# Self attention on one Trainium2 core: a table of orders, one for each batch, block and position

## The chip, the cores and the metric

The kernel runs on one core of one Trainium2 chip. The metric is the device time of one execution in microseconds. All data are 32-bit floats.

## The reference

A decoder block reads `x` (2 x 2048 x 512) and a short encoded context (2 x 77 x 512). Cut to what matters here:

```python
sb = _rel_bias(dec_rel_self, Tt, Tt) + causal        # bias by distance, and the causal mask
y = tgt
yn = _ln(y, dec_n1_s, dec_n1_b)
y = y + _mha(yn, yn, dec_sa_in_w, dec_sa_in_b, dec_sa_out_w, dec_sa_out_b, sb)   # self attention
y = y + _mha(_ln(y, dec_n2_s, dec_n2_b), memory, ...)                            # cross attention
h = _ln(y, dec_n3_s, dec_n3_b)
y = y + (relu(h @ dec_ff1_w.T + dec_ff1_b) @ dec_ff2_w.T + dec_ff2_b)

# in _mha, 16 heads of 32:
scores = einsum('bhqd,bhkd->bhqk', q, k) / sqrt(hd) + bias
attn = softmax(scores, axis=-1)
out = einsum('bhqk,bhkd->bhqd', attn, v)
```

The change touches the self attention alone: causal, two batches, 2048 positions, 16 heads.

## The kernel before

**Units.** The self attention is cut into 128 *units* `(b, m, g, t)`: batch `b`, block `m` of 512 queries, group `g` of four heads, and position `t`, one of four tiles of 128 queries in the block. A unit's queries see `m * 4 + t + 1` tiles of 128 keys, so the blocks grow: a unit of `m = 0` has 1 to 4 key tiles, one of `m = 3` has 13 to 16. Units run in order, `t` fastest, `b` slowest.

**What a unit does.** (1) *Scores* (`scores`, L375): in *pieces* of up to four key tiles, TensorE multiplies queries and keys. The four heads of the group use 32 rows of the array each, side by side, and each head has a PSUM bank of its own, so a piece takes four banks. VectorE moves each bank to SBUF and takes the row maximum on the way (L384, and L391 for the last two key tiles, which get the bias). (2) *Exponentials* (L406): one ScalarE instruction for each head, when the whole row is there. (3) *Transposes* (`turn`, L427): for each key tile TensorE transposes the four heads' probabilities into one bank, and ScalarE (L434) or VectorE (L432) copies the bank to `pts`, a ring of eight tiles. (4) *Values* (`values`, L456): TensorE multiplies the transposed probabilities and the values, each head in 32 columns of the array, into a bank that is taken out of the ring for as long as the sum is open. L469 (ScalarE) copies the sum to `oT`, or L471 (VectorE) adds it there, if the unit's key tiles come in more than one half.

**Banks.** PSUM's eight banks are one ring (`bank()`): whoever needs a bank gets the one used longest ago, and waits until that one has been emptied.

**Slots.** Between the units stands other work in *slots*: `slot(n)` runs the functions in `light[n]` (loads, normalizations, reciprocals of sums, transposes of the input at L305 with ScalarE's copies at L310), then the products in `jobs[n]` (queries, keys, values and the output's projection: L215, L226, L239, and in pieces L1049, L1134, with VectorE's sums at L1056 to L1065, L1150, L1164), then `late[n]`. Each job first asks for the next weights, three to four jobs ahead. In batch 1, blocks 0 and 1, the slots also hold the first piece of the cross attention (L811 to L883).

**What sets the order.** The scheduler is off (`tc.manual_schedule()`): each engine executes in the order in which the program's text issues. A main loop goes through the stream of score pieces. In each turn it takes a unit's next one or two pieces and issues: their transposes; a fixed number of exponentials of the next unit, by block; with the unit's last pieces, the slot of the next unit; one or two score pieces of the unit after the next, if `may_score()` says that their place in SBUF is free (two units share the buffer `pp`, one growing from each end); the values. The rules are the same for both batches, and for all positions but for some counts:

```python
            third = units[n][1] == 2
            if third and ends:
                exps(2)
            if ends and n + 1 < end:
                slot(n + 1)
            if not third:
                exps((0, 2, 1, 1)[units[n][1]])
            if may_score():
                if units[n][1] and (len(pair) > 1 or third):
                    score_two()
                else:
                    score_next()
```

After the units come the rest of the cross attention and the feed-forward part, whose lines (L1638, L1667, L1758, L1801) the change does not touch.

## Time and profile before

| | |
|---|---|
| time, median of 3 runs | 2726.79 us (2725.84 to 2729.86) |
| profiled execution: span | 2726.8 us; the page gives no time outside the span |
| busy: TensorE, its weight loads | 2708.1 us (99%), 2217.9 us (81%) |
| busy: VectorE, ScalarE, GpSimd | 1839.9 (67%), 1537.0 (56%), 1002.4 us (37%) |
| self attention (all units) | 0 to about 1640 us of the span |
| granted TensorE clock, mean | 0.997 |
| DMA | 385.10 MB, mean 141 GB/s |

A matmul counts as busy from its start to the modelled end of its result, so matmuls that follow each other overlap, and a busy TensorE is not one that works at its peak. On TensorE's rows of 32-bit matmuls each instruction but a transpose leaves two records. The blocks of the self attention begin at 0 (b = 0, m = 0), 161.6, 369.6, 589.5 (m = 1, 2, 3), 853.5 (b = 1, m = 0), 989.7, 1184.2 and 1404.3 us (m = 1, 2, 3), counted by the first transpose of a block.

### The profile page before, as it was taken

The numbers are of one execution on the slowest core, as the hardware profiler recorded it, in microseconds if no ns is written. First come the engines' busy times: TensorE is split into PE (matmuls) and PEld (weight loads), VectorE is DVE, ScalarE is ACT, GpSimd is POOL, SyncE is SP. The second block draws the span as 40 slices with busy tenths as digits, with TensorE's granted clock in tenths as the row PEclk, the third lists the DMA queues.
The fourth block names the chain that finished last, engine by engine and source line by source line (L and its number), as shares of the span: only waits on it lengthen the run. The fifth ranks groups of instructions, "written<-read, shape, count | busy, mean of one in ns | idle before, by whom it ended". The sixth has DMA issues, their size and how long they took to land.

```text
span 2726.8 us, 68267 instructions
## 1 busy us (share of the span) xinstructions
PE 2708.1 (99%) x26606; PEld 2217.9 (81%) x26606; DVE 1839.9 (67%) x5445; ACT 1537.0 (56%) x2978; POOL 1002.4 (37%) x844
## 2 busy tenths in 40 slices
PE   9999999999999999999999999999999999999998
PEld 6678877777876677777777777898989898989898
DVE  4776688888885677788888783646464746464645
ACT  3554567777786547667777784444444444444431
POOL 2612235500300513322300203455556565656456
PEclk9999999999999999999999999999999999999999
DMA  8724355511213522343311206565657565656465
GB/s 242 213 92 135 126 155 164 168 50 43 67 45 89 143 76 72 111 133 98 126 50 35 79 19 220 171 214 173 213 171 239 168 216 170 218 166 219 151 224 185
DMA packets 296277, 385.10 MB, mean 141 GB/s; under 512 B 41184, under 2 KB 165648, under 8 KB 295826
## 3 DMA queue, kind: packets, MB, share of 16 engines
q1 hardware_dynamic: 295954, 380.73, 44.1%
q8 instruction: 211, 3.46, 0.5%
q14 instruction: 112, 0.92, 0.1%
HBM read 334.15 MB, written 46.47 MB: 140 GB/s over the span
## 4 chain that ended last, share of the span: by engine, by line
PE 95%; DVE 1%; ACT 1%; DMA 1%; POOL 1%; issue 1%; SPq 0%; DVEq 0%; POOLq 0%; ACTq 0%
PE psum L427 18%; PE psum L1638 14%; PE psum L1667 13%; PE psum L375 11%; PE psum L456 9%; PE psum L1134 8%; PE psum L1801 3%; PE psum L1758 3%; PE psum L1049 3%; PE psum L866 2%; PE psum L836 1%; PE psum L874 1%; PE psum L590 1%; PE psum L811 1%; PE psum L239 1%; PE psum L215 1%
## 5 line engine op out<-in xcount | busy, mean ns | idle before, releaser
L406 ACT ACTIVATE pp<-pp,nm 128x128 f32<-128x128 f32 (+15 forms) x512 | 611.8, 1200 | 28.6 <-DVE nm L401 27.8
L384 DVE TENSOR_SCALAR_CACHE_REDUCE pp<-psum 128x512 f32<-128x512 f32 (+3 forms) x1024 | 556.2, 591 | 51.3 <-PE psum L375 49.7
L434 ACT COPY pts<-psum 128x512 f32<-128x512 f32 x714 | 384.1, 594 | 312.6 <-PE psum L427 265.6
L427 PE MATMUL psum<-ident,pp 128*128 128x128 f32 x4352 | 530.4, 277 | 4.7 <-ACT nT L310 4.0
L427 PEld LDWEIGHTS psum<-ident,pp 128*128 128x128 f32 x4352 | 474.0, 141 | 55.7 <-DVE pp L384 21.4
L375 PE MATMUL psum<-kT,q 32*128 32x512 f32 (+3 forms) x2560 | 336.5, 559 | 2.5 <-DVE q L217 1.0
L456 PEld LDWEIGHTS psum<-pts,vv 128*32 128x32 f32 x8704 | 226.4, 110 | 127.4 <-DVE pp L384 55.4
L1667 PE MATMUL psum<-pp 128*128 128x128 f32 x2560 | 304.5, 276 | 1.9 <-POOL pp L962 1.6
L1667 PEld LDWEIGHTS psum<-pp 128*128 128x128 f32 x2560 | 296.3, 192 | 8.6 <-issue 2.8
L432 DVE COPY pts<-psum 128x512 f32<-128x512 f32 x374 | 245.2, 685 | 82.6 <-PE psum L427 80.3
L456 PE MATMUL psum<-pts,vv 128*32 128x128 f32 x8704 | 279.6, 276 | 0.8 <-DVE mx L391 0.3
L962 POOL TENSOR_TENSOR pp<-pp 128x512 f32<-128x512 f32 x159 | 212.8, 1356 | 111.0 <-DMA pp<-in_dec_ff_wT_dram 50.6
L1638 PE MATMUL psum<-vv,pp 128*128 128x256 f32 x1024 | 236.2, 381 | 0.0
L375 PEld LDWEIGHTS psum<-kT,q 32*128 32x128 f32 x2560 | 146.3, 183 | 107.1 <-issue 41.3
L1638 PEld LDWEIGHTS psum<-vv,pp 128*128 128x128 f32 x1024 | 190.3, 190 | 25.8 <-issue 0.5
L391 DVE CUSTOM_DVE_ANT_0 pp<-psum,bias 128x256 f32<-128x256 f32 (+1 forms) x512 | 196.0, 411 | 19.7 <-PE psum L375 19.7
L1651 DVE TENSOR_TENSOR kT<-kT,psum 128x512 f32<-128x512 f32 x96 | 65.8, 686 | 191.6 <-PE psum L1638 191.4
L1654 ACT ACTIVATE kT<-kT,vecs 128x256 f32<-128x256 f32 x192 | 86.9, 501 | 156.6 <-DVE kT L1651 155.9
L1638 PE MATMUL psum<-nT,pp 128*128 128x256 f32 x768 | 174.1, 380 | 0.5 <-DVE oT L471 0.5
L1638 PEld LDWEIGHTS psum<-nT,pp 128*128 128x128 f32 x768 | 144.2, 190 | 20.8 <-issue 1.4
L1675 ACT COPY oT<-psum 128x128 f32<-128x128 f32 x56 | 15.0, 268 | 238.9 <-PE psum L1667 238.9
L494 POOL TENSOR_TENSOR oT<-rirows,oT 128x512 f32<-128x512 f32 x30 | 38.4, 1280 | 293.6 <-DMA rirows<-rec 181.7
(272 smaller groups left out, 4110.6 us busy)
## 6 DMA issues: line engine op xcount, KB each, us to landing
pp<-w_d SPq DMA_DIRECT2D x520, 256.0 KB
pp<-in_dec_ff_wT_dram SPq DMA_DIRECT2D x112, 256.0 KB
bias<-tzg SPq DMA_DIRECT2D x128, 128.0 KB
pp<-wo_d SPq DMA_DIRECT2D x56, 256.0 KB
wqk<-in_dec_sa_in_wT_dram SPq DMA_DIRECT2D x52, 256.0 KB
wqk<-sa_q SPq DMA_DIRECT2D x84, 128.0 KB
vv<-in_enc_ff_wT_dram SPq DMA_DIRECT2D x8, 1024.0 KB
xr<-in_x_dram SPq DMA_DIRECT2D x32, 256.0 KB
```

Of the source, the lines that this page charges most:

```text
L375: nc.tensor.matmul(banks[r][:, : kn * P], q[rows4(r), ts(t, P)], kT[rows4(r), g, k0 * P : (k0 + kn) * P], start=True, stop=True,)
L384: nc.vector.tensor_scalar(p[:, k0 : k0 + far], s[:, :far], 1.0, None, ALU.mult, ALU.max, accum_out=st["mx"][:, r, c : c + 1],)
L391: nc.vector.tensor_tensor_reduce(p[:, k0 + far : i + 1], s[:, far:kn], near[:, 2 - (kn - far) :], 1.0, LOWEST, ALU.add, ALU.max, accum_out ...
L406: nc.scalar.activation(p, p, AF.Exp, bias=nm, accum_out=to)
L427: nc.tensor.transpose(pt[:, ts(x, P)], state[n]["p"][r][:, k], ident)
L432: nc.vector.tensor_copy(pts[:, : len(load), :], pt[:, :w])
L434: nc.scalar.copy(pts[:, : len(load), :], pt[:, :w])
L456: nc.tensor.matmul(ot[rows4(r)], vv[:, k, ts(g * HC + r, HD)], got.pop((n, k, r)), start=k == k0 and (whole or not begun), stop=k == k1 - ...
L962: engine.tensor_tensor(out, a, b, ALU.subtract)
L1134: nc.tensor.matmul(mm[:, ts(f, TOK)], left[:, c, ts(f, P)], right[:, c, :], start=c == 0, stop=c == 1,)
L1638: nc.tensor.matmul(mm[:, ts(f, TOK)], a[:, c, ts(f, P)], b[:, c, :], start=fresh and f == 0 and c == 0, stop=c == 1, skip_group_check=True,)
L1667: nc.tensor.matmul(psum[:, bank_i, ts(col, P)], lhs[:, c, :], w[:, c, :], start=fresh and k in (0, 3) and c == 0, stop=c == 3, skip_group_ ...
```

## The change

The main loop's rules are replaced by a table. For each batch, each block from `m = 1` on and each position `t` a line of letters is the order in which the unit is issued: `a` and `d` transpose the next key tile and copy it on ScalarE or VectorE; `E` issues one exponential of the next unit; `S` one score piece, where its place is free, the second piece of a row first if both are; `V` multiplies what was transposed by the values and closes the sum; `v` does that and leaves the sum open in its bank; `J` issues what is left of the next slot and `j` only its front (`light`). `slot` is split into parts for that. Blocks `m = 0` keep their order, and the last two units have one made by a rule (`script_of`). `turn` takes one tile and the engine that copies it; `values` takes a list of key tiles and whether the sum closes. `may_score` also looks at the places in `pp` that are still held (`held_by`, `leave`). No computation is added or left out but for this: 18 transposed tiles more are copied by VectorE and 18 fewer by ScalarE, and 15 additions of value sums on VectorE (L471) are gone, since batch 0's block 3 keeps its sums open between the halves.

In the new text the transposes are L417, the values L441, the copies L423 (ScalarE), the sums' copy L454, the slots' products L1035 and L1120, and the cross attention's L822, L860, L869.

*Place 1: TensorE in batch 0, block m = 3, heads' group 2, from the slot inside the unit t = 0 to the scores inside t = 1.* Before:

```order
L1134 MATMUL psum<-wqk,oT 128x256 x4
L375 MATMUL psum<-kT,q 128x384 x4
L375 MATMUL psum<-kT,q 128x512 x4
L456 MATMUL psum<-pts,vv 32x128 x20
L427 MATMUL psum<-ident,pp 128x128 x32
L375 MATMUL psum<-kT,q 128x512 x8
L456 MATMUL psum<-pts,vv 32x128 x32
L427 MATMUL psum<-ident,pp 128x128 x24
L305 MATMUL psum<-ident,xt 128x128 x4
L375 MATMUL psum<-kT,q 128x512 x8
L456 MATMUL psum<-pts,vv 32x128 x24
```

and in the changed kernel:

```order
L1120 MATMUL psum<-wqk,oT 128x256 x4
L375 MATMUL psum<-kT,q 128x512 x4
L441 MATMUL psum<-pts,vv 32x128 x20
L375 MATMUL psum<-kT,q 128x384 x4
L417 MATMUL psum<-ident,pp 128x128 x32
L375 MATMUL psum<-kT,q 128x512 x8
L441 MATMUL psum<-pts,vv 32x128 x32
L417 MATMUL psum<-ident,pp 128x128 x24
L375 MATMUL psum<-kT,q 128x512 x4
L305 MATMUL psum<-ident,xt 128x128 x4
L441 MATMUL psum<-pts,vv 32x128 x24
L375 MATMUL psum<-kT,q 128x512 x4
```

The pair of pieces behind the slot's products (L1134, L305) is split: one piece stands ahead of the values, or of the slot, and the other behind the values. The pair behind 32 transposes stays a pair.

*Place 2: ScalarE at the same units (from the exponentials inside t = 1 on).* Before:

```order
L406 ACTIVATE pp,sums<-pp,nm 128x15x128 x2
L469 COPY oT<-psum 128x128
L434 COPY pts<-psum 128x512 x3
L406 ACTIVATE pp,sums<-pp,nm 128x15x128
L310 ACTIVATE nT<-psum,vecs 128x128 x4
L406 ACTIVATE pp,sums<-pp,nm 128x15x128
L434 COPY pts<-psum 128x512 x6
```

and in the changed kernel:

```order
L406 ACTIVATE pp,sums<-pp,nm 128x15x128 x2
L423 COPY pts<-psum 128x512 x3
L406 ACTIVATE pp,sums<-pp,nm 128x15x128 x2
L310 ACTIVATE nT<-psum,vecs 128x128 x4
L454 COPY oT<-psum 128x128
L423 COPY pts<-psum 128x512 x6
```

Both exponentials now stand ahead of the copies of the slot's transposes (L310), and the unit's value sum is copied once, at its end.

*Place 3: TensorE in batch 1, block m = 1, group 0, inside the unit t = 0 and on to the values inside t = 1.* Before:

```order
L375 MATMUL psum<-kT,q 128x384 x4
L375 MATMUL psum<-kT,q 128x512 x4
L456 MATMUL psum<-pts,vv 32x128 x20
L427 MATMUL psum<-ident,pp 128x128 x24
L883 MATMUL psum<-vv,kT 128x512 x4
L836 MATMUL psum<-pp 128x77 x16
L1134 MATMUL psum<-wqk,xt 128x256 x4
L1134 MATMUL psum<-wqk,nT 128x256 x4
L375 MATMUL psum<-kT,q 128x512 x8
L456 MATMUL psum<-pts,vv 32x128 x24
```

and in the changed kernel:

```order
L375 MATMUL psum<-kT,q 128x384 x4
L375 MATMUL psum<-kT,q 128x512 x4
L441 MATMUL psum<-pts,vv 32x128 x20
L869 MATMUL psum<-vv,kT 128x512 x4
L822 MATMUL psum<-pp 128x77 x16
L1120 MATMUL psum<-wqk,xt 128x256 x4
L1120 MATMUL psum<-wqk,nT 128x256 x4
L417 MATMUL psum<-ident,pp 128x128 x24
L375 MATMUL psum<-kT,q 128x512 x4
L441 MATMUL psum<-pts,vv 32x128 x24
L375 MATMUL psum<-kT,q 128x512 x4
```

The slot's four groups of products come ahead of the unit's transposes instead of behind them; the scores no longer stand behind the slot, and their second piece comes behind the values.

Over the whole self attention TensorE's list holds the same instructions. It has 195 runs of score pieces before and 246 after, and 192 runs of values in both; TensorE goes from full-array work (transposes, products) to tiled work (scores, values, the cross attention's heads) 200 times before and 228 times after. In the blocks from `m = 1` on, of 158 runs of scores before, 66 are pairs behind a slot's products, 58 are pairs behind transposes and 34 are single pieces; of 209 after, 5, 68 and 136.

The diff, cut to its core (of the table four lines are shown):

```diff
-        def turn(pieces):
-
-            first = units[pieces[0][0]][1] == 0
...
-                free = pieces[0][0] == len(units) - 2 and (pieces[0][1] or o >= 4)
-                if free or (o % 2 if first else o in (4, 6) if len(loads) == 8 else o >= (len(loads) + 1) // 2):
-                    nc.vector.tensor_copy(pts[:, : len(load), :], pt[:, :w])
-                else:
-                    nc.scalar.copy(pts[:, : len(load), :], pt[:, :w])
-                if not first and o == (7 if len(loads) == 8 else min(3, len(loads) - 1)):
-                    exps(1)
-            exps(HC if first else 0 if units[pieces[0][0]][1] == NMB - 1 else 1)
+        def turn(load, by):
...
+            if by == "d":
+                nc.vector.tensor_copy(pts[:, : len(load), :], pt[:, :w])
+            else:
+                nc.scalar.copy(pts[:, : len(load), :], pt[:, :w])
...
-            keep = t < TB - 1 if whole else (g, t) == (2, 0) and k1 <= i
+            keep = t < TB - 1 if whole else not closes or (g, t) == (2, 0) and not ends
...
+            return [front] + [lambda k=k, run=run: job(k, run) for k, (_, run, _) in enumerate(jobs[n])] + [back]
...
+        SCRIPTS = {
+            (0, 1, 0): 'a a a d E d S E J E E S S V S',
...
+            (0, 3, 1): 'a a a a d a d a E E S S v S a a a d E d d S E J V S',
...
+            (1, 1, 1): 'J a a S a d d E d J E E E S V S S',
...
+            (1, 3, 2): 'j a a a a a d a d E E S S V S a a a a E d d E d J S S V S',
...
+        def may_score(ahead=0):
+
+            if at[0] + ahead >= len(stream):
+                return False
+            n, k0, kn = stream[at[0] + ahead]
+            if any(k in held_by for k in places(n, k0, kn)):
+                return False
...
+            for step in script_of(n):
+                if step in ("a", "d"):
+                    k = to_turn.pop(0)
+                    turn([(n, k, r) for r in range(HC)], step)
+                    turned.append(k)
+                    assert len(turned) <= pts_all.shape[1]
+                    leave(n, k)
+                elif step == "E":
+                    exps(1)
+                elif step == "J":
+                    while parts:
+                        parts.pop(0)()
+                elif step == "j":
+                    parts.pop(0)()
+                elif step == "S" and may_score() and stream[0][0] <= n + 2:
+                    two = stream[0][1] == 0 and may_score(1) and stream[1][0] == stream[0][0]
+                    score_next(1 if two else 0)
+                elif step in ("v", "V"):
+                    values(n, turned, not to_turn, step == "V")
+                    turned = []
```

More of the change, by code (lines that the diff above doesn't have):

```diff
@@ L1891, in tile_encoder_decoder @@
         slot(0)
[L1892 to L1896 removed]
+        for n in range(end):
+            b, m, g, t = units[n]
+            while scored_to[n] != size[n]:
                 score_next()
```

151 lines of the change are left out of this document (69 added, 82 removed), and 20 rows, old and new, of the table SCRIPTS.

## The prediction

> **What bounds the kernel now.** I read the page first, then the windows of the eight blocks, then the score line alone in the same windows, and last TensorE in order of time. The page:
>
> ```profile
> span 2726.8 us, 68267 instructions
> PE 2708.1 (99%) x26606; PEld 2217.9 (81%) x26606; DVE 1839.9 (67%) x5445; ACT 1537.0 (56%) x2978; POOL 1002.4 (37%) x844
> ```
>
> TensorE is the bound, and 99% leaves no idle time to win. But a matmul counts as busy until its result is out, and several overlap, so a wait shorter than that hides inside "busy". The question is how much of the 2708 us is waiting in disguise, in the part that the change reorders. The profiled execution's span is the median of the runs (2726.8 against 2726.79 us), so the sum is made against 2726.8.
>
> Four of the six blocks that are reordered (second column: length; then PE, PEld, DVE, ACT, POOL busy; clock; DMA share; GB/s):
>
> ```profile
> 161.60:369.60 208.00, 207.47 (x2090) 168.88 (x2089) 145.67 (x514) 111.95 (x232) 50.28 (x40) 1.00 0.39 124
> 369.60:589.50 219.90, 219.80 (x2657) 171.37 (x2656) 182.30 (x625) 160.15 (x276) 84.81 (x71) 1.00 0.48 144
> 589.50:853.50 264.00, 263.55 (x3426) 206.83 (x3420) 206.40 (x688) 206.76 (x323) 30.81 (x24) 1.00 0.16 48
> 989.70:1184.20 194.50, 194.43 (x2052) 147.20 (x2048) 145.78 (x499) 128.63 (x267) 55.62 (x47) 0.99 0.29 91
> ```
>
> The clock is full. VectorE, which empties the score banks, is at most 83% busy (182.30 of 219.90), ScalarE 78% (206.76 of 264.00): neither is the bound of a block, so what TensorE waits for there is a matter of order, not of rate. The score line alone in the same windows (all eight blocks; the first and fifth are the blocks m = 0, which keep their order):
>
> ```profile
> 0.00:161.60 161.60, 19.85 (x160) 8.18 (x160) 0.99 0.69 201
> 161.60:369.60 208.00, 34.19 (x273) 15.52 (x272) 1.00 0.39 124
> 369.60:589.50 219.90, 50.47 (x401) 21.53 (x400) 1.00 0.48 144
> 589.50:853.50 264.00, 61.51 (x464) 27.51 (x464) 1.00 0.16 48
> 853.50:989.70 136.20, 17.88 (x144) 7.06 (x144) 0.97 0.47 133
> 989.70:1184.20 194.50, 42.50 (x276) 18.15 (x272) 0.99 0.29 91
> 1184.20:1404.30 220.10, 50.55 (x401) 21.53 (x400) 1.00 0.32 105
> 1404.30:1640.00 235.70, 59.55 (x448) 26.85 (x448) 1.00 0.16 52
> ```
>
> The blocks m = 1 of the two batches do the same scores with the same number of matmuls, yet cost 34.19 and 42.50 us: eight microseconds of waiting in one block, with PE shown 99% busy. TensorE in order of time tells where (start, length, engine, group; a score piece is 8 matmul records, two for each head):
>
> ```profile
> 373.11 1.14 PE L375 MATMUL psum<-kT,q 32*128 32x512 f32 x8
> 374.18 1.74 PE L456 MATMUL psum<-pts,vv 128*32 128x128 f32 x56
> ...
> 741.18 2.77 PE L375 MATMUL psum<-kT,q 32*128 32x384 f32 x16
> 743.88 1.30 PE L456 MATMUL psum<-pts,vv 128*32 128x128 f32 x40
> 745.11 3.71 PE L427 MATMUL psum<-ident,pp 128*128 128x128 f32 x32
> 748.75 2.00 PE L375 MATMUL psum<-kT,q 32*128 32x512 f32 x16
> 750.68 1.96 PE L456 MATMUL psum<-pts,vv 128*32 128x128 f32 x64
> 752.56 2.84 PE L427 MATMUL psum<-ident,pp 128*128 128x128 f32 x24
> 755.24 0.60 PE L305 MATMUL psum<-ident,xt 128*128 128x128 f32 x4
> 755.77 2.09 PE L375 MATMUL psum<-kT,q 32*128 32x512 f32 x14
> 758.19 1.12 PE L375 MATMUL psum<-kT,q 32*128 32x512 f32 x2 [0.34 <-ACT nT L310]
> 759.24 1.52 PE L456 MATMUL psum<-pts,vv 128*32 128x128 f32 x48
> ```
>
> **The price of a run of scores.** From start to the next group's start, two 512-wide pieces in one run take 750.68 - 748.75 = 1.93, one alone 374.18 - 373.11 = 1.07. So a piece costs 0.86 and a run 0.21 more, once, however long it is. In busy time (2.00 and 1.14) the piece is 0.86 too and the run 0.28. Narrower pieces are taken in proportion: 0.645 (384 wide), 0.43, 0.215.
>
> **How much of the score line is waiting.** Its groups by width:
>
> ```profile
> L375 PE MATMUL psum<-kT,q 32*128 32x512 f32 x1600 | 240.1, 616 | 1.6 <-DVE q L217 1.0 <-ACT nT L310 0.3
> L375 PE MATMUL psum<-kT,q 32*128 32x384 f32 x448 | 58.2, 524 | 0.0
> L375 PE MATMUL psum<-kT,q 32*128 32x256 f32 x448 | 44.1, 426 | 0.6 <-DVE kT L1164 0.5
> L375 PE MATMUL psum<-kT,q 32*128 32x512 f32 (+3 forms) x2560 | 336.5, 559 | 2.5 <-DVE q L217 1.0 <-DVE kT L1164 0.5 <-ACT nT L310 0.5
> L427 PE MATMUL psum<-ident,pp 128*128 128x128 f32 x4352 | 530.4, 277 | 4.7 <-ACT nT L310 4.0 <-DVE wbig L1150 0.2
> ```
>
> The last row is the transposes, for later. The first three, divided by 8, are 200 pieces of 512, 56 of 384, 56 of 256, and of the remaining 64 records 8 of 128: 172.0 + 36.1 + 24.1 + 1.7 = 233.9 us. TensorE's order has 195 runs of scores: 195 x 0.28 = 54.6. Undisturbed it would be 288.5; the row has 336.5. So **48 us are waits**. The two windows m = 0 hold 19.85 + 17.88 = 37.7: their 38 pieces (304 records; one of each width in each of eight groups, 17.2, and six of the next blocks, 3.5) and 37 runs (10.4) account for 31.1, so 6.6 us wait there. **41.4 us wait in the six blocks that are reordered.**
>
> They sit in one place. Of the 158 runs of those blocks, 66 are pairs right behind the products of a slot, 58 are pairs behind transposes and 34 are single pieces. The pair at 748.75, behind transposes, waits for nothing. The pair at 741.18 (384 and 512 wide, behind products) takes 2.70 where 0.645 + 0.86 + 0.21 = 1.72 are due: 0.98 of waiting. That at 755.77 takes 3.47 for 1.93. What held it stands on ScalarE:
>
> ```profile
> 754.74 1.92 ACT L406 ACTIVATE pp<-pp,nm 128x1920 f32<-128x1920 f32 x1
> 756.63 1.51 ACT L310 ACTIVATE nT<-psum,vecs 128x128 f32<-128x128 f32 x4
> ```
>
> The eight banks go round in turn. A pair needs all eight, the last being that of the product issued just ahead; here that bank is emptied by L310, queued behind an exponential, until 758.14, and the last score starts at 758.19. I put all 41.4 us on the 66 pairs, 0.63 each.
>
> **The change, part by part.**
>
> *Splitting the pairs (the gain).* In the new order 5 pairs stand behind products, 68 behind transposes, and 136 pieces are alone: ahead of the slot, ahead of the values or behind them. A single piece takes the four oldest banks, and its partner comes after the values or the slot, at least 1.2 us later (the L456 rows). 5 x 0.63 = 3.2 us stay; the 68 pairs wait for nothing. For a single piece the ends are nothing, as at 373.11, and what the row below shows, a piece of 256 behind values:
>
> ```profile
> 1170.88 0.92 PE L375 MATMUL psum<-kT,q 32*128 32x256 f32 x8
> ```
>
> It is busy 0.92 for 0.43 + 0.28 = 0.71: 0.21 of waiting. It comes third behind a pair, when VectorE is four banks further behind than it will be in the new order, so I take the middle, 0.10: 13.6 us for 136 (0 to 28.6). Left are 16.8, and 41.4 - 16.8 = **24.6 us go**.
>
> *More runs (the price).* 209 runs instead of 158: 51 x 0.21 = 10.7. And 28 more times TensorE leaves full-array work for a tiled one: 32 transposes ended by scores take 748.75 - 745.11 = 3.64, 24 ended by other transposes 755.24 - 752.56 = 2.68, which is 3.57 for 32, so 0.07 each time, 2.0 in all. **Price 12.7 us**, certain, because nothing hides work on TensorE itself. The values keep their 192 runs.
>
> *Copies, sums, exponentials.* 18 transposed tiles more are copied by VectorE, and 15 additions of value sums go, because batch 0's last block keeps its sums in a bank across both halves:
>
> ```profile
> L434 ACT COPY pts<-psum 128x512 f32<-128x512 f32 x714 | 384.1, 594 | 312.6 <-PE psum L427 265.6
> L432 DVE COPY pts<-psum 128x512 f32<-128x512 f32 x374 | 245.2, 685 | 82.6 <-PE psum L427 80.3
> L471 DVE TENSOR_TENSOR oT<-psum,oT 128x128 f32<-128x128 f32 x60 | 16.9, 282 | 3.6 <-PE psum L456 2.6 <-ACT pp L406 0.9
> ```
>
> VectorE: 18 x 0.685 - 15 x 0.282 = +8.1 us over six blocks; ScalarE: -18 x 0.594 = -10.7. With a sixth of VectorE idle in its fullest block this costs nothing; without that cover it would be 8.1 us. The held bank leaves seven to the ring between the halves; a single piece and a slot's product still find theirs free.
>
> *Slots moved ahead.* In batch 1, block m = 1, each slot's products, loads and normalizations come before the transposes rather than behind them. The loads keep their place among the jobs, and once started the distance from slot to slot is as before; only the first slot comes sooner, by a run of transposes (2.8 to 3.7 us in the L427 rows). Late weights there would cost at most that, once; I take nothing. What is queued behind: VectorE's sums of the products, which the next transposes need not wait for, since ScalarE copies most of the first ones. This is the block with 8 us more waiting than its twin, and the place of the largest single gain.
>
> **Sum.** -24.6 + 12.7 = -11.9: 2726.8 - 11.9 = **2715 us**. With the single pieces' ends, 0 and 0.21, it is 2701 and 2729.
>
> **The rivals.**
>
> *The singles find every bank free.* The gain is 38.2, net 25.5: **2701**. For it: 373.11, and that a single piece needs only banks that are long done. Against: exponentials of up to 1.9 us now stand closer to a slot's copies on ScalarE in batch 0's last block. 0.17.
>
> *The gain is eaten by its price.* If the lone pieces wait 0.21 as at 1170.88, 31.8 us stay, 9.6 go, and 12.7 are paid: **2729**, no change that shows (a measurement of this kernel cannot tell under 0.2%, 5.5 us, from none). 0.19.
>
> *The waits are a matter of rate, and stay.* VectorE frees a 512-wide bank in 0.61 us while TensorE fills four in 0.86. If the order of the pieces does not matter to that backlog, the 41 us turn up elsewhere, at the transposes behind a late piece above all, which then find their banks still held. Then only the price is left: **2739**. It decides the sign once fewer than 12.7 of the 41 us go. Against it stands VectorE's idle sixth, and the pairs behind transposes that wait for nothing. 0.13.
>
> ```profile
> 750.52 0.69 DVE L384 TENSOR_SCALAR_CACHE_REDUCE pp<-psum 128x512 f32<-128x512 f32 x1
> 751.13 0.08 DVE L384 DVE_READ_ACCUMULATOR pp<-psum 128x1 f32 x1
> 751.13 0.69 DVE L384 TENSOR_SCALAR_CACHE_REDUCE pp<-psum 128x512 f32<-128x512 f32 x1
> ```
>
> The Trainium skill, in TensorEngine Tiling (Array Packing), section "PSUM Bottleneck", holds that after tiling has sped TensorE up fourfold the emptying of PSUM may become the limit; by that rule this last case would be the likeliest. The windows do not bear it out for whole blocks, only for the microseconds after a pair.
>
> **How the numbers follow.** The forecast has 0.51 (2706 to 2721), the three rivals 0.17, 0.19, 0.13. Faster by over 0.2%: 0.51 + 0.17 = 0.68; within 0.2%: 0.19; slower: 0.13. The range reaches from 2695, below the first rival because the few waits of transposes and products might go as well, to 2735, halfway into the last. The likeliest case's own range is 2706 to 2721.
>
> **What would show it.** In the changed profile the score line, 336.5 us now, should be 233.9 + 246 x 0.28 + 6.6 + 16.8 = 326 busy; 313 speaks for the first rival, 341 for the second, 351 for the third unless the waits have moved to the transposes, whose 530.4 us (L427) would then grow by more than 5. The window of batch 1's block m = 1 should lose the most. The forecast is wrong if a lone piece behind values waits as long as the pair did, if transposes behind it do, or if a run costs more than 0.21.

## The result and the profile after

The changed kernel takes **2707.1 us** (median of 4 executions, 2705.3 to 2708.4); the kernel before, run beside it on the same chip, 2727.6 (2725.8 to 2729.9). The ratio is **0.9921, with a 95% interval of 0.9907 to 0.9935**: faster by 0.8%, 20.5 us. The forecast was 2715 with a range of 2695 to 2735.

The first lines of the page of the changed kernel; its profiled execution has a span of 2706.3 us:

```profile
span 2706.3 us, 68257 instructions
PE 2684.3 (99%) x26606; PEld 2199.2 (81%) x26606; DVE 1848.9 (68%) x5448; ACT 1526.2 (56%) x2960; POOL 1002.3 (37%) x844
```

TensorE is 99% busy as before, and the span is 20.5 us shorter: what went was "busy" time. The score line alone in the windows of the blocks behind the first, the borders again at the first transpose of a block (second column: length; then PE busy, PEld busy, clock, DMA share, GB/s):

```profile
164.20:371.10 206.90, 33.28 (x273) 11.12 (x272) 1.00 0.40 124
371.10:589.20 218.10, 50.00 (x400) 19.21 (x400) 1.00 0.49 146
589.20:847.40 258.20, 57.18 (x468) 21.98 (x464) 1.00 0.17 50
847.40:990.00 142.60, 19.02 (x144) 7.48 (x144) 0.99 0.50 136
990.00:1169.10 179.10, 35.67 (x272) 14.40 (x272) 1.00 0.32 94
1169.10:1387.50 218.40, 48.93 (x404) 21.53 (x400) 1.00 0.34 104
1387.50:1620.00 232.50, 57.10 (x448) 24.02 (x448) 1.00 0.17 53
```

Against the windows before, the largest falls are in batch 1's block m = 1 (42.50 to 35.67 us) and in batch 0's block m = 3 (61.51 to 57.18). The border between batch 1's blocks m = 0 and m = 1 has moved, because in block m = 1 the slot now comes ahead of the first transpose. The two together last 142.6 + 179.1 = 321.7 us, where they lasted 136.2 + 194.5 = 330.7: 9.0 us less. Batch 0's block m = 3 lost 5.8 us (264.0 to 258.2), batch 1's 3.2 (235.7 to 232.5; its ends, 1640 and 1620, are set by hand).

The groups of the scores and the transposes (busy, mean ns of one, idle time ahead of them and what ended it):

```profile
L375 PE MATMUL psum<-kT,q 32*128 32x512 f32 (+3 forms) x2560 | 320.3, 565 | 2.2 <-ACT kT L231 1.4 <-DVE kT L1150 0.5 <-ACT nT L310 0.2
L417 PE MATMUL psum<-ident,pp 128*128 128x128 f32 x4352 | 527.4, 276 | 5.7 <-ACT nT L310 4.0 <-ACT pp L406 1.3 <-DVE wbig L1136 0.2
```

The score line fell by 16.2 us of busy time (336.5 to 320.3), though it has 51 runs more. The transposes did not take the waits over; they fell by 3.0. TensorE in order of time, at the place that the prediction quoted (batch 0, block m = 3, group 2):

```profile
741.36 3.71 PE L417 MATMUL psum<-ident,pp 128*128 128x128 f32 x32
745.00 2.00 PE L375 MATMUL psum<-kT,q 32*128 32x512 f32 x16
746.93 1.95 PE L441 MATMUL psum<-pts,vv 128*32 128x128 f32 x64
748.82 2.84 PE L417 MATMUL psum<-ident,pp 128*128 128x128 f32 x24
751.59 1.14 PE L375 MATMUL psum<-kT,q 32*128 32x512 f32 x8
752.66 0.66 PE L305 MATMUL psum<-ident,xt 128*128 128x128 f32 x4
753.24 1.52 PE L441 MATMUL psum<-pts,vv 128*32 128x128 f32 x48
754.69 1.14 PE L375 MATMUL psum<-kT,q 32*128 32x512 f32 x8
```

and ScalarE beside it:

```profile
752.88 1.90 ACT L406 ACTIVATE pp<-pp,nm 128x1920 f32<-128x1920 f32 x1
754.67 0.20 ACT L406 ACTIVATION_READ_ACCUMULATOR pp<-pp,nm 128x1 f32 x1
754.76 1.51 ACT L310 ACTIVATE nT<-psum,vecs 128x128 f32<-128x128 f32 x4
```

The slot's copies (L310) still stand behind an exponential, and here end at 754.76 + 1.51 = 756.27, later against the transposes of the slot than before. But neither piece needs that bank: the first starts ahead of the slot, the second behind the values, and the first takes the undisturbed 1.07 us (752.66 - 751.59), the second the same 1.14 of busy time. In the kernel before, the pair took 3.47 us at this place for work of 1.93.

**Where the 20.5 us come from.** I went through all groups of TensorE from start to the next group's start and took off what each needs undisturbed: its columns at the pace of an undisturbed pair of scores (1.73 us, which is 1.93 less 0.20 for entering; with four heads at once the pair streams as many columns as 16 transposes, so 32 of them are put at 3.46), 0.20 us for entering a run of scores, 0.15 for one of values or of the cross attention, and 0.09 for leaving transposes or products for tiled work. What remains I call waits, in us over the whole self attention. At this pace an undisturbed run of 32 transposes (3.55) already counts as 0.09 us of waiting, in both kernels alike, so the differences say more than the levels:

| | before | changed | difference |
|---|---|---|---|
| waits in runs of scores | 51.4 | 20.4 | -31.0 |
| waits in transposes | 33.7 | 27.6 | -6.1 |
| waits in values | 4.0 | 1.7 | -2.3 |
| waits in products and cross attention | 8.2 | 14.3 | +6.1 |
| entering and leaving runs | 88.7 | 101.6 | +12.9 |

Together -20.4; that this is the difference of the spans follows from the way of counting. The last row is a count of runs times the fixed prices above, not a measured time. About half of the +6.1 is the start: the first transpose came at 30.8 us of the span instead of 27.6, behind the first loads, where nothing was changed. In the traces of the experiments it comes at 27.7 to 28.9, so these 3 us belong to this one execution.

In the six blocks with a table the runs of scores group like this (number, waits in us in all, mean):

| | before | changed |
|---|---|---|
| pair behind a slot's products | 66, 36.1, 0.55 | 5, 1.8, 0.36 |
| pair behind transposes | 58, 3.8, 0.07 | 68, 6.7, 0.10 |
| piece alone | 34, 3.7, 0.11 | 136, 4.7, 0.035 |

### The profile page after: what moved, and what is told of

It is laid out like the page before. It is cut to its first block, busy times and chain, and to the rows that moved or that the text cites. A ratio compares the mean times of both kernels' runs of the same rounds, so it can differ in the third digit from the quotient of the medians.

```text
span 2706.3 us, 68257 instructions
## 1 busy us (share of the span) xinstructions
PE 2684.3 (99%) x26606; PEld 2199.2 (81%) x26606; DVE 1848.9 (68%) x5448; ACT 1526.2 (56%) x2960; POOL 1002.3 (37%) x844
## 3 DMA queue, kind: packets, MB, share of 16 engines
q8 instruction: 211, 3.46, 0.5%
## 4 chain that ended last, share of the span: by engine, by line
PE 96%; DVE 1%; ACT 1%; DMA 1%; POOL 1%; SPq 0%; issue 0%; DVEq 0%; POOLq 0%; ACTq 0%
PE psum L417 18%; PE psum L1636 15%; PE psum L1665 13%; PE psum L375 11%; PE psum L441 9%; PE psum L1120 8%; PE psum L1799 3%; PE psum L1756 3%; PE psum L1035 3%; PE psum L852 2%; PE psum L822 1%; PE psum L860 1%; PE psum L576 1%; PE psum L797 1%; PE psum L239 1%; PE psum L215 1%
## 5 line engine op out<-in xcount | busy, mean ns | idle before, releaser
L406 ACT ACTIVATE pp<-pp,nm 128x128 f32<-128x128 f32 (+15 forms) x512 | 611.4, 1200 | 23.4 <-DVE nm L401 23.2
L423 ACT COPY pts<-psum 128x512 f32<-128x512 f32 x696 | 374.4, 593 | 346.3 <-PE psum L417 309.5
L417 PE MATMUL psum<-ident,pp 128*128 128x128 f32 x4352 | 527.4, 276 | 5.7 <-ACT nT L310 4.0
L417 PEld LDWEIGHTS psum<-ident,pp 128*128 128x128 f32 x4352 | 475.2, 141 | 64.5 <-issue 21.4
L441 PEld LDWEIGHTS psum<-pts,vv 128*32 128x32 f32 x8704 | 225.7, 110 | 119.4 <-DVE pp L384 49.3
L375 PE MATMUL psum<-kT,q 32*128 32x512 f32 (+3 forms) x2560 | 320.3, 565 | 2.2 <-ACT kT L231 1.4
L421 DVE COPY pts<-psum 128x512 f32<-128x512 f32 x392 | 257.7, 686 | 84.8 <-PE psum L417 81.3
L441 PE MATMUL psum<-pts,vv 128*32 128x128 f32 x8704 | 278.0, 275 | 1.1 <-DVE pp L384 0.8
L391 DVE CUSTOM_DVE_ANT_0 pp<-psum,bias 128x256 f32<-128x256 f32 (+1 forms) x512 | 196.0, 411 | 13.2 <-PE psum L375 12.7
L375 PEld LDWEIGHTS psum<-kT,q 32*128 32x128 f32 x2560 | 127.5, 183 | 87.3 <-issue 50.0
```

Source lines behind the costliest of these rows:

```text
L375: nc.tensor.matmul(banks[r][:, : kn * P], q[rows4(r), ts(t, P)], kT[rows4(r), g, k0 * P : (k0 + kn) * P], start=True, stop=True,)
L391: nc.vector.tensor_tensor_reduce(p[:, k0 + far : i + 1], s[:, far:kn], near[:, 2 - (kn - far) :], 1.0, LOWEST, ALU.add, ALU.max, accum_out ...
L406: nc.scalar.activation(p, p, AF.Exp, bias=nm, accum_out=to)
L417: nc.tensor.transpose(pt[:, ts(x, P)], state[n]["p"][r][:, k], ident)
L421: nc.vector.tensor_copy(pts[:, : len(load), :], pt[:, :w])
L423: nc.scalar.copy(pts[:, : len(load), :], pt[:, :w])
```

## The experiments

All are the changed kernel with other rows in its table; nothing of the computation is left out. The letters are those of the table. All ratios are to the kernel before, run on the same chip.

### Pairs joined again, all else as changed

In every row with a split pair, the second `S` moves ahead of the values again, and pieces issued ahead of a slot go behind it. 197 runs of scores, 35 of them pairs behind products.

```diff
-            (0, 3, 1): 'a a a a d a d a E E S S v S a a a d E d d S E J V S',
+            (0, 3, 1): 'a a a a d a d a E E S S v S a a a d E d d E J S S V S',
...
-            (1, 1, 1): 'J a a S a d d E d J E E E S V S S',
+            (1, 1, 1): 'J a a a d d E d E E E S S V S',
```

> The changed kernel with every split pair of score pieces joined again ahead of the values; copies, exponentials and slots keep their new places. 197 runs of scores in place of 246, 35 pairs behind products in place of 5. If the splits earn the time: 49 runs fewer give back 49 x 0.21 + 29 x 0.07 = 12.3 us, 30 pairs more behind products wait 0.55 to 0.63 each, 16 to 19 us; so 4 to 7 us slower than the changed kernel, 2711 to 2714. If the splits earn nothing and the new places of slots and exponentials do: only the price comes back, 2695.

Measured: 2725.8 us, 0.9995 (0.9986 to 1.0004). The direction is that of the first theory, the size is not: 18.7 us over the changed kernel where 4 to 7 were expected. The whole gain is gone. The score line, and TensorE at the same place once more:

```profile
L375 PE MATMUL psum<-kT,q 32*128 32x512 f32 (+3 forms) x2560 | 333.9, 560 | 5.4 <-ACT nT L310 2.9 <-ACT kT L231 1.4 <-DVE kT L1150 0.5
```

```profile
758.13 0.60 PE L305 MATMUL psum<-ident,xt 128*128 128x128 f32 x4
758.66 2.09 PE L375 MATMUL psum<-kT,q 32*128 32x512 f32 x12
762.96 1.84 PE L375 MATMUL psum<-kT,q 32*128 32x512 f32 x4 [2.21 <-ACT nT L310]
764.72 2.44 PE L441 MATMUL psum<-pts,vv 128*32 128x128 f32 x48
```

The pair takes 764.72 - 758.66 = 6.06 us for 1.93, the longest wait of a run of scores in this trace. The reason for this one stands on ScalarE:

```profile
759.52 1.90 ACT L406 ACTIVATE pp<-pp,nm 128x1920 f32<-128x1920 f32 x1
761.40 1.51 ACT L310 ACTIVATE nT<-psum,vecs 128x128 f32<-128x128 f32 x4
```

L310 ends at 762.91, and the seventh of the pair's eight heads starts at 762.96. The changed kernel has both exponentials ahead of L310, so the bank comes later than before. Batch 0's block m = 3 waits 17.7 us in its scores here, 8.9 in the kernel before and 0.3 in the changed one. The 35 pairs behind products wait 24.8 us, 0.71 each (5 with 1.8 us in the changed kernel), and the 87 pairs behind transposes 16.6 us (68 with 6.7).

But the pair above is not typical of the block. The other 11 pairs behind products there wait 0.9 to 1.3 us each, 11.4 together, and for something else. One of them, and VectorE's first eviction of its own scores:

```profile
744.01 2.82 PE L375 MATMUL psum<-kT,q 32*128 32x512 f32 x16
745.17 0.69 DVE L384 TENSOR_SCALAR_CACHE_REDUCE pp<-psum 128x512 f32<-128x512 f32 x1 [0.30 <-PE psum L375]
```

The eviction ends at 745.86, and the pair's last head starts at 745.92; in all 11 it starts about 0.06 us behind an eviction of the pair's own first scores. This block keeps its value sum open (`v`), so the ring has seven banks, and a pair of eight has to wait until its own first bank is empty. The pairs are thus joined here in a ring that is too short for them, which the kernel before had in a single unit of a block. So this run shows that the held bank and the earlier exponentials are good only together with the splits; how much the splits earn by themselves, it doesn't show. The next run does.

### Only the pairs split

The rows of the old order, with copies, exponentials, slots and closing sums as in the kernel before, and nothing new but `S V S` for `S S V S`.

```diff
-            (0, 3, 1): 'a a a a d a d a E E S S v S a a a d E d d S E J V S',
+            (0, 3, 1): 'a a a a d a d a E E S S V a a a d E d d J E S V S',
```

> The old order of copies, exponentials and slots written as rows of the table, with one thing changed: every pair behind a slot's products is split, one piece ahead of the values and one behind them (267 runs of scores, no pair behind products). If the splits earn the time: 36 to 41 us of waits go but some 3 to 6, 72 runs more cost 15.1; 2707 to 2713. If the slots' and exponentials' new places earn it: the price alone, 2743.

Measured first: 2741.4 us, 1.0059 (1.0046 to 1.0071), what the rival had said, but not for its reason. The score line fell as expected, to 324.3 us of busy time. What grew were the transposes, in two places of each batch:

```profile
L417 PE MATMUL psum<-ident,pp 128*128 128x128 f32 x4352 | 536.9, 279 | 25.7 <-ACT pp L406 22.5 <-ACT nT L310 2.8 <-DVE wbig L1136 0.2
```

```profile
384.29 1.39 PE L375 MATMUL psum<-kT,q 32*128 32x512 f32 x8
388.08 0.33 PE L417 MATMUL psum<-ident,pp 128*128 128x128 f32 x1 [2.40 <-ACT pp L406]
389.42 0.33 PE L417 MATMUL psum<-ident,pp 128*128 128x128 f32 x1 [1.02 <-ACT pp L406]
```

At the end of the blocks m = 1 the next block's rows have a third score piece, for which my rows had no place; `may_score` let it through only a unit later, the row was complete too late, and its exponentials came directly ahead of the unit's own transposes, which waited for each of them. The cause is an error of my table, not the split. With a place for the third piece at the ends of the blocks m = 1 and m = 2,

```diff
-            (0, 1, 3): 'a a a a d a d a E E J E E S V S',
+            (0, 1, 3): 'a a a a d a d a E E J E E S V S S S',
```

> The old order of copies, exponentials and slots with only the pairs behind products split, as in the run before that cost 24 us at transposes in the two blocks m = 2, but with places for the third piece of scores that the last two units of a group issue at a block's end. 263 runs of scores. If the splits alone carry the change: 36 us of waits go but some 4 to 8, 68 runs more cost 14.3; 2707 to 2713, and the transposes fall back from 537 to 530 busy. If the new places of slots and exponentials are needed as well: 2717 or more.

Measured: **2706.4 us, 0.9918 (0.9904 to 0.9931)**, the changed kernel's time. Its transposes and scores:

```profile
L417 PE MATMUL psum<-ident,pp 128*128 128x128 f32 x4352 | 524.2, 276 | 5.5 <-ACT nT L310 4.0 <-ACT pp L406 1.1 <-DVE wbig L1136 0.2
L375 PE MATMUL psum<-kT,q 32*128 32x512 f32 (+3 forms) x2560 | 323.6, 567 | 2.3 <-ACT kT L231 1.4 <-DVE kT L1150 0.5 <-ACT nT L310 0.2
```

So one rule, a pair behind products is split, carries the whole of the change. All else in the table together earns nothing that can be measured: this kernel has 17 runs of scores more than the changed one, but goes from full-array work to tiled work 28 times less. 87 lone pieces behind products wait 3.4 us here, 0.04 each.

### Every pair split

The changed kernel, but in the blocks m = 2 and m = 3 the pairs behind transposes are split too: 56 runs more.

```diff
-            (1, 2, 1): 'a a d a a d a E d E E S S V E E S d E a E E J S S V',
+            (1, 2, 1): 'a a d a a d a E d E E S V S E E S d E a E E J S S V',
```

> The changed kernel with the pairs behind transposes split too, one piece ahead of the values and one behind (302 runs of scores in place of 246; 12 pairs left of 68). These pairs hardly wait, so this is the price by itself: 56 x 0.21 = 11.8 us, less the 0 to 5 us that they did wait; 2714 to 2719. If a run of its own costs nothing when its neighbours hide it, or if splitting always helps: 2702 to 2707.

Measured: 2730.0 us, 1.0013 (1.0004 to 1.0022): 22.9 more than the changed kernel (19.8 between the two profiled spans), beyond both expectations. The score line pays the price as it was held to be:

```profile
L375 PE MATMUL psum<-kT,q 32*128 32x512 f32 (+3 forms) x2560 | 334.8, 574 | 2.2 <-ACT kT L231 1.4 <-DVE kT L1150 0.5 <-ACT nT L310 0.2
```

334.8 - 320.3 = 14.5 us busy for 56 runs, 0.26 each, where the prediction had 0.28 (0.21 from start to start, 11.8 us). The rest is one new wait. Among the waits of TensorE by releaser there are now three rows on the copy of a value sum, of which the changed kernel has none (us in all, times, longest):

```profile
PE psum L1035 <- ACT oT L454: 3.7, 2, 1.9
PE psum L305 <- ACT oT L454: 1.9, 1, 1.9
PE psum L1120 <- ACT oT L454: 1.6, 1, 1.6
```

These 7.2 us all fall in batch 1's block m = 2, in units t = 2. There the piece that was moved behind the values takes four more banks ahead of the slot, so that the slot's first product is the eighth to ask behind the value sum and gets that sum's bank; its copy (L454) is queued behind four exponentials on ScalarE. Start to start this counts 8.5 us more in that block (12.8 instead of 4.3, with the transposes that stand ahead of the product). A split costs 0.21 us and shifts what is queued where; it pays only where a pair waits.

### The slot's place in batch 1, block m = 1

The changed kernel with the old rows in this block, pairs split.

```diff
-            (1, 1, 1): 'J a a S a d d E d J E E E S V S S',
+            (1, 1, 1): 'a a a d E d d E J E E S V S',
```

> The changed kernel with batch 1's block m = 1 in the old order of copies, exponentials and slots (the slot behind the transposes again), but with its pairs split. 252 runs of scores. If splitting is what removes the waits there: within 2 us of the changed kernel, 2705 to 2709. If the slot's place ahead of the transposes is what does: the 8 us that this block had above its twin of batch 0 come back, 2713 to 2717.

Measured first: 2713.6 us, 0.9953 (0.9941 to 0.9966). It looked as if the slot's place earned 6.5 us, but the table lacked the same place for the third piece: transposes sat idle 4.6 us for the exponentials (L406), against 1.3 in the changed kernel. With the place added to the rows of t = 2 and t = 3:

> The changed kernel with batch 1's block m = 1 in the old order (slot behind the transposes), its pairs split, and with places for the third piece at the block's end, which the first try lacked. If splitting removes the waits there: 2705 to 2709. If the slot's place ahead of the transposes does: 2712 to 2715.

Measured: 2706.0 us, 0.9919 (0.9905 to 0.9932), the time of the changed kernel. The slot's place earns nothing that shows.

### The held bank, and the engines of the copies

Batch 0's block m = 3 with `V` for `v`, so that each half closes its sum and the 15 additions come back:

```diff
-            (0, 3, 0): 'a a a a d a d a E E S S v S a a a d E d J S E V S',
+            (0, 3, 0): 'a a a a d a d a E E S S V S a a a d E d J S E V S',
```

> The changed kernel with batch 0's block m = 3 closing its value sums after each half (the 15 additions on VectorE come back, and the ring has its eighth bank between the halves). If the held bank and the additions cost nothing, as forecast: 2705 to 2709. If VectorE's additions stand in the way of score banks: 15 x 0.28 = 4 us, 2711. If the eighth bank is what TensorE lacks there: below 2705.

Measured: 2706.1 us, 0.9919 (0.9905 to 0.9932). And each copy on the engine that had it before, `a` and `d` exchanged in 16 rows:

```diff
-            (1, 2, 2): 'a a a a a d d a E E E S S E V E S d d a E E E J S S V',
+            (1, 2, 2): 'a a a a d a d a E E E S S E V E S a a d E E E J S S V',
```

> The changed kernel with each tile's copy on the engine that made it before (18 copies go back from VectorE to ScalarE); all else stays. If the engine of the copies costs nothing, as forecast: 2705 to 2709. If VectorE's 8.1 us more were on the path: 2699. If the new choice of engines is a part of the gain: 2712 or more.

Measured: 2708.2 us, 0.9932 (0.9919 to 0.9946). Both cost nothing that can be told from the changed kernel.

### No pair behind products, and none split

If only the products just ahead made a pair wait, moving the slot would do as well as splitting, without its price. In all six blocks the slot goes ahead of the unit's transposes; pairs stay together.

```diff
-            (0, 2, 1): 'a a a a a d a d E E S S E V S E a d E E E E J S V S',
+            (0, 2, 1): 'J a a a a d a d a E E S S E V E a d S V S S',
```

> No pair is split, but no pair stands behind a slot's products either: in all six blocks the slot comes ahead of the unit's transposes, and the pair of score pieces follows the transposes. Engines of the copies as in the kernel before. 199 runs of scores instead of 246. If a pair waits only because a bank of the products just ahead of it is still full, the pairs now wait as those behind transposes did (0.065 us each in the kernel before), the 47 runs fewer give back about 47 x 0.21 = 10 us of price, and the time is 2697 to 2701 us: a better change than the one made. If a pair waits because it needs eight banks at once, whatever stands ahead of it (16 pairs behind transposes in block m = 1 of batch 1 waited 8.2 us, 0.5 each, in the run with the pairs joined), about 60 moved pairs wait 0.3 to 0.5 each, 18 to 30 us, and the time is 2715 to 2722 us.

Measured: **2758.1 us, 1.0108 (1.0091 to 1.0125)**. Both expectations fail, the second by size: 51 us over the changed kernel. Runs of scores wait 77.2 us instead of 20.4. 120 pairs behind transposes wait 39.6 us, 0.33 each, at the low end of what the second theory had; and 34 lone pieces, of which neither theory had spoken, wait 30.1, 0.89 each. TensorE in a unit of block m = 2:

```profile
451.26 2.00 PE L375 MATMUL psum<-kT,q 32*128 32x512 f32 x16
453.19 1.95 PE L441 MATMUL psum<-pts,vv 128*32 128x128 f32 x64
455.07 1.09 PE L417 MATMUL psum<-ident,pp 128*128 128x128 f32 x8
456.10 1.86 PE L375 MATMUL psum<-kT,q 32*128 32x512 f32 x8
458.45 0.65 PE L441 MATMUL psum<-pts,vv 128*32 128x128 f32 x16 [0.49 <-ACT pts L423]
```

and the evictions on VectorE, the first and the eighth of the pair and the copy behind them:

```profile
452.42 0.69 DVE L384 TENSOR_SCALAR_CACHE_REDUCE pp<-psum 128x512 f32<-128x512 f32 x1 [0.80 <-PE psum L375]
...
456.70 0.69 DVE L384 TENSOR_SCALAR_CACHE_REDUCE pp<-psum 128x512 f32<-128x512 f32 x1
457.31 0.69 DVE L421 COPY pts<-psum 128x512 f32<-128x512 f32 x1
```

The pair goes in within 2 us and takes VectorE from 452.42 to 457.31, 4.9 us, to empty: eight banks at 0.61 us. The lone piece comes at 456.10, 4.8 us behind the start of the pair, and its four banks become free one by one; it takes 2.35 us for 1.07. The last 0.49 of this is another queue: the values behind the piece wait for a copy (L423) that ScalarE has behind an exponential. The values' group shows that second part over the whole kernel:

```profile
L441 PE MATMUL psum<-pts,vv 128*32 128x128 f32 x8704 | 281.7, 276 | 19.5 <-ACT pts L423 15.9 <-DVE pp L384 2.7 <-DVE pts L421 0.2
```

Read from the ends of the waits, 24 of the 34 lone pieces, those that start 4.8 to 5.7 us behind the start of a pair, have 30.0 of the 30.1 us: 12.6 in the pieces themselves, until VectorE has emptied a bank, and 17.4 at the values behind them, until ScalarE has made a copy. In the kernel before, the slot stood between the first half's values and this piece and gave both engines time.

### The slot between the pair and the lone piece

To see whether that time is what lacks, the one kernel moves one step of the last: in blocks m = 2 the slot stands behind the first half's values.

```diff
-            (0, 2, 1): 'J a a a a d a d a E E S S E V E a d S V S S',
+            (0, 2, 1): 'a a a a d a d a E E S S E V E J a d S V S S',
```

> The run with the slot ahead of the transposes, with one step moved in blocks m = 2: the slot stands between the values of a unit's first half and the transposes of its second. No run of scores more or less (199), and the lone piece still stands behind transposes; but the slot's products, 3.5 us and more, now lie between the pair and the lone piece. If the lone piece waited because VectorE was still emptying the pair's eight banks, the 34 lone pieces wait 0.1 us or less instead of 0.89 (30 us in all), the products that stood behind them some 10 us less, and the time falls from 2758 to 2715 to 2725 us. If they waited because of what is queued on ScalarE (copies of the transposed tiles behind exponentials), the lone pieces keep at least half of their wait and the time is 2740 to 2760 us.

Measured: 2731.8 us, 1.0016 (1.0007 to 1.0025), 26 us less by moving one letter in eight rows. The spans of the two profiled executions differ by 33 us (2758.8 and 2725.6); the executions scatter more here than elsewhere, from 2727.5 to 2734.0. The place, and the values' group:

```profile
440.41 2.00 PE L375 MATMUL psum<-kT,q 32*128 32x512 f32 x16
442.33 1.95 PE L441 MATMUL psum<-pts,vv 128*32 128x128 f32 x64
444.22 1.99 PE L1120 MATMUL psum<-wqk,oT 128*128 128x256 f32 x8
446.05 1.89 PE L1120 MATMUL psum<-wqk,xr 128*128 128x256 f32 x8
447.78 1.04 PE L417 MATMUL psum<-ident,pp 128*128 128x128 f32 x8
448.74 1.14 PE L375 MATMUL psum<-kT,q 32*128 32x512 f32 x8
```

```profile
L441 PE MATMUL psum<-pts,vv 128*32 128x128 f32 x8704 | 279.4, 275 | 6.2 <-DVE pp L384 2.7 <-ACT pts L423 2.5 <-DVE pts L421 0.2
```

The lone piece comes 8.3 us behind the start of the pair and waits for nothing; all 34 wait 4.9 us instead of 30.1, products and the cross attention 8 less, transposes 7 more. Without these 7 the time would lie at the upper end of the 2715 to 2725 that the first theory gave. The slot gives time to both queues, so this run does not part VectorE's share from ScalarE's. The 120 pairs behind transposes still wait 34.1 us, and time since the scores ahead is not what they lack: 36 of them start 10 us or more behind those and wait 13.1 us, while in the kernel before 58 at 5 to 9 us waited 3.8. The bank that they wait for can be read from the trace. Of the 70 that wait over 0.15 us (33.7 us together), the last head of 50 (24.0 us) starts 0.05 to 0.07 us behind the end of a copy of a transposed tile by VectorE (L421), and that of 8 (2.2 us) so behind one by ScalarE (L423).

### The best block of each order

The split alone, with batch 1's blocks m = 1 and m = 2 from the changed kernel, since waits and entries of these blocks added up to less there.

```diff
-            (1, 1, 1): 'a a a d E d d E J E E S V S',
+            (1, 1, 1): 'J a a S a d d E d J E E E S V S S',
```

> The old order with only the split of the pairs, but blocks m = 1 and m = 2 of batch 1 as in the changed kernel: for each block the order whose waits and price added up to less in the traces. If these differences between the blocks (about 1 to 3 us each) belong to the orders, 2702 to 2706 us. If they belong to the execution (start-up, loads), the time is that of the split alone, 2706 to 2708 us.

Measured: **2703.0 us (2701.3 to 2703.8), 0.9907 (0.9892 to 0.9922)**, the lowest median of all. Its interval overlaps that of the split alone and that of the changed kernel, so whether the 3.4 us below the split alone are real stays open. In the traces block m = 1 of batch 1 has some 3 us less of waits and entries with the changed rows; with the old rows in the changed kernel (the second run on the slot's place) no such loss showed.

## Why the prediction was right, and where it was off

**The direction and its cause: right.** The 48 us of waiting inside a "99% busy" TensorE were there (51.4 from start to start), sat for the most part on the pairs behind products, and went when these were split. From start to start the 66 pairs waited 0.55 us each, the prediction had 0.63 in busy time. Splitting alone brings the whole gain.

**The price: as forecast.** Forecast 12.7 us; the account has 12.9 (88.7 to 101.6). Both are the same counts times nearly the same prices, so this agreement tests little. What tests the price is that an undisturbed pair takes 1.93 us and an undisturbed piece 1.07 in the changed kernel too, and that the 56 further runs of the kernel with every pair split cost 0.26 busy each, against 0.28.

**The term that was mis-sized: the wait of a lone piece.** The prediction took 0.10 us between bounds of 0 and 0.21; the 136 wait 0.035 each, 4.7 us instead of 13.6, 8.9 less. The bound came from a third piece that follows a pair and its values directly; that place occurs four times in the kernel before (0.36 us each from start to start) and never in the changed one, in the six blocks. "The 68 pairs wait for nothing" was off the other way: 6.7 us, of which 3.8 had been there before. Pairs behind products kept 1.8 us instead of 3.2. In these blocks 43.6 us of waiting became 13.3, so 30.3 went where 24.6 were forecast. With the 0.7 us that went in the blocks m = 0, that is 31.0: **6.4 us more gain**.

**What was taken as nothing.** Waits in transposes (-6.1) and values (-2.3) fell as well, and those at the start, in the products and in the cross attention grew (+6.1): 2.3 us more. So 11.9 + 6.4 + 2.3 - 0.2 for the price = 20.4. The prediction had named this for its lower end ("the few waits of transposes and products might go as well"). At 2707.1 the result lies inside the likeliest case's own range, 2706 to 2721, but near its lower end, 7.9 us from the forecast.

**The tests that were named.** The score line was to become 326 busy; it became 320.3, between the forecast and the first rival's 313, and far from 341 and 351. The transposes were not to grow by more than 5; they fell by 3.0. Batch 1's block m = 1 was to lose the most; with the block ahead of it, whose border moved, it did, by 9.0 us.

**Copies, sums, held bank, slots: nothing, as forecast.** VectorE's busy time grew by 9.0 us (forecast 8.1), ScalarE's fell by 10.8 (10.7), and exchanging the engines or closing the sums moved the time by no more than 1.1 us. The held bank is free only because no pair is issued while it is held: with the pairs joined, 11 of them waited 11.4 us for a bank of their own. The slot's place in batch 1's block m = 1, which the prediction counted as the place of the largest gain, has it because of its splits; the place by itself earned nothing that shows.

**The rivals.** The first (2701) was the nearest in its mechanism: lone pieces do find nearly every bank free; of its 14 us over the forecast 8 came. The second falls with the 0.035 us (it was written as 2729; its own terms, 9.6 gone and 12.7 paid, give 2729.9). The third, a matter of rate, falls for this change: the waits did not turn up elsewhere. The Trainium skill's rule beside it (TensorEngine Tiling (Array Packing), section "PSUM Bottleneck") does not decide whole blocks here, where VectorE is at most 87% busy (190.53 of 218.40, batch 1's block m = 2):

```profile
1169.10:1387.50 218.40, 216.62 (x2661) 171.76 (x2657) 190.53 (x634) 154.59 (x265) 55.93 (x44) 1.00 0.34 104
```

But the 4.9 us that VectorE needs for a pair's banks count: in the order that puts the next scores into them (the slot ahead of all transposes, 51 us slower) the lone pieces there wait 30 us.

**Which bank a pair waits for.** The prediction's account, that it is the bank of the product just ahead, can be checked pair by pair: the last head starts 0.05 to 0.07 us behind the end of the instruction that empties its bank. In the kernel before, 50 pairs behind products wait over 0.15 us. In 44 of them (30.4 of 35.2 us) that instruction empties a bank that the slot has filled, 40 times on VectorE and 4 times on ScalarE. So the account holds for most, but the place that the prediction quotes, with L310 on ScalarE behind an exponential, is the exception: it is VectorE's queue that most pairs wait for. In 2 pairs it is a copy of a transposed tile. In the last 4, of 0.98 us each, it is VectorE's eviction of the pair's own first scores (L391). One of these is the pair at 741.18, which the prediction quotes as a wait for products: VectorE is through with the products at 742.04, and the last head starts at 742.83. It stands in group 2, t = 0, of block m = 3, the one kind of unit in which the kernel before keeps a sum open too, and the ring has seven banks. The account is also too narrow: without any product ahead, pairs still waited 0.33 us each, most of them for VectorE's copy of a transposed tile.

## What to carry to other kernels

Where banks go round in a ring, a burst that needs the whole ring waits until the bank that was filled last ahead of it has been emptied, and where something holds a bank back, until its own first one has. Split it where it waits, with other work of TensorE between the halves, and leave it whole where it doesn't: each split has a price that one row of the profile tells. Behind a burst that stays whole, leave the engines the time to empty it (here eight banks at 0.61 us, over about 6 us from the start of the pair): lone pieces behind values and transposes waited at 4.8 to 5.7 us, and 13 such pieces of the changed kernel, at 6.0 to 7.5 us, waited 0.3 us in all. And count the place of every piece when an order is written out by hand, since one piece without a place moved all the exponentials behind it.

## What the runs showed of the hardware

**A busy TensorE tells nothing here.** Kernels from 2703 to 2758 us show PE 99% busy, and one of 2741 shows 98%. The slowest shows 99% as well, with some 128 us of waits by the account from start to start, twice those of the changed kernel (64):

```profile
PE 2720.4 (99%) x26606; PEld 2241.5 (81%) x26606; DVE 1843.6 (67%) x5447; ACT 1530.9 (55%) x2976; POOL 1001.0 (36%) x844
```

The busy share of the weight loads, which the Trainium skill (Perfetto Trace Analysis, section "Identifying the Most-Contended Engine") advises to use instead for judging how close a kernel is to its limit, tells these kernels apart no better: 81% in the slowest kernel, in the changed one and in the one before. Only starts against undisturbed work of the same size showed the waits.

**Entering row-tiled work has a price of its own**: 0.21 us for each run from start to start, 0.26 to 0.28 in busy time. One undisturbed 512-wide piece takes 1.07 us in the trace of every kernel run here, and a pair 1.93 in every one that has an undisturbed pair. Leaving full-array work costs 0.07 to 0.09 more: 32 transposes take 3.64 us ahead of scores and 3.55 ahead of products. The Trainium skill (TensorEngine Tiling (Array Packing), section "Key Properties") states that a change of the tiling mode drains TensorE, without a figure; 56 runs more at 14.5 us are in line with it.
